# Tokens turned by VectorE and moved through DRAM instead of turned by TensorE, with the products of values as the last work of a slot

## The chip, the cores and the metric

The kernel runs on one core of a Trainium2 chip. Its time is the device time of one execution in microseconds; of several executions the median is given. The engines have separate in-order queues of instructions: TensorE (PE, with its weight loads as PEld), VectorE (DVE), ScalarE (ACT), GpSimd (POOL), and SyncE (SP), which here only issues transfers. Semaphores order instructions of different engines.

## The reference, cut to what matters

The input `x` holds 16 sequences of 256 tokens with 256 features, in float32. An attention layer and a gated feed-forward layer follow one another, each between two layer norms and with a residual:

```python
x = x + _layernorm(_L0_attn_ref(_layernorm(x), Wq, Wkv, Wkvh, Wg, Wout))
x = x + _layernorm(_L0_ffn_ref(_layernorm(x), w_gate_up, w_proj))
```

The attention has 16 heads of 128. Queries come from `Wq`; keys and values have one common part of 128 columns each (`Wkv`), which every head multiplies by its own factor per token. These factors come from `Wkvh` and, through cumulated products of sigmoids, from `Wg`, and are summed along the sequence. Queries and keys are rotated (RoPE), the scores are scaled, masked causally and put through a softmax, and the outputs of all heads go through `Wout`. The feed-forward layer multiplies by ternary weights (gate and up, 1024 hidden columns each), takes silu(gate) * up, an RMS norm, and a second ternary product.

Before both layers a product needs the normalised tokens with features along the partitions. Tokens arrive with tokens along the partitions, so they are transposed: this is the work that the change concerns.

## The kernel before, in words

Two sequences make a pair, so there are 8 pairs (class `Pair`), 16 heads each (class `Head`): 128 heads in all. Class `After` is one sequence's work after its heads: projection by `Wout`, norm, residual, feed-forward, norm, residual.

The order of all work is written out by hand. `slot(g)` (L1271) is one step for head g. It issues, in this order: steps planned for the place "first"; a load of `kh`, the factors of head g + 4 (`fetch`); the division of head g - 1's probabilities by their sums (`divide`, ScalarE, tile `even`); the scores of head g with mask and exponential (`scores`: TensorE `sps`, VectorE mask, ScalarE exponential); the turn of head g - 1's probabilities (`turn`, L631); the keys of head g + 2 (`keys`, POOL, `kT`); the queries of head g + 1 (`queries`, TensorE, `qps`); the scaled values of head g - 1 (`scale_values`, POOL, `vph`); place "scored"; the rotation of the queries of head g + 1 (VectorE: two halves of sines `turned_q`, cosines in place in `qps`, sum into `qT`); place "turned"; the reciprocals of head g's sums; place "projection"; the products of values of head g - 2 (`outputs`, TensorE, `ops`, and ScalarE's copy `oT`); places "emptied" and "last". A slot below is counted from the start of its scores on TensorE; slot 5 of a repeat of 16 means g with g mod 16 = 5.

The turn of probabilities shows the method that the change takes over for tokens. `turn` lets VectorE transpose blocks of 32x32 (`sq`), SyncE writes the result to DRAM (`moved`), and four reads, each for 32 partitions, bring the blocks where a full transposition has them (`pT`).

Everything that isn't a head's own is put into the places by `plan` methods. `Pair.plan` (L492) begins (from pair 2 on) two slots before the previous pair's first head, at slot 14 of a repeat, with `moments` (VectorE, bn_stats of `xt`), `normalise` (POOL, `xn_a`), `transpose` (TensorE, `tp_a`, into one of the four rotating PSUM buffers) and `keep` (ScalarE, into `xnT`); from `xnT` come the factors `hg` (slot 2, "last"), keys `kp` (slot 3) and values. `hg` feeds ScalarE's `gates`, first thing of slot 3. The key rotation `turned_k`, `kr` is in slot 5. `After.plan` (L1007) is called with slot 6 of a repeat for the even sequence and with slot 0 of the next one for the odd sequence: `moments`, `normalise` (`xn_f`), two slots later `transpose` (`tp_f`) and `split` (ScalarE rounds into `xhi`, VectorE subtracts into `xlo`). Then follow gates, ups and projections by `wproj_sb` (`ffn`) in the next slots, put mostly at "last" and "scored". `plan_after` (L1036) puts the projection by `Wout` (`att`), the moments of `att` (slot 3, "emptied"), the factors on POOL (slot 4, "first") and the residual: ScalarE's `y` (`add`) and POOL's sum (`add_done`, `xt`) in slots 4 to 6.

Pools: `p2` has two buffers per tag (`xn`, `sq32`, `xhi`, `xlo`, `vph`), `ps_mm` four PSUM buffers of one tag for `sps`, `qps`, `tp`, `hg`, `kp`, `gps`, `ups`, and `ps_o` one for `ops`. The last three sequences (`late`) are handled by `end` after the last slot.

Of the kernel before, what the change touches and what calls it, by code (L numbers as in the profile page):

```python
# [16 lines left out]
P = 128  # L17
# [6 lines left out]
BP = 2  # L24
# [16 lines left out]
def sandwich_kernel(  # L41
# [180 lines left out]

    class Rows:
# [35 lines left out]
        def apply(self, dst, src, engine):  # L259
            for t in range(self.count):  # L260
                engine.tensor_scalar(
                    dst[:, t, :],
                    src[:, t, :],
                    self.mv[:, t, 0:1],
                    self.rs[:, t : t + 1],
                    ALU.subtract,
                    ALU.mult,
                )

# [59 lines left out]
    class Pair:  # L329
# [7 lines left out]
        def normalise(self, b):  # L337
            self.xn[b] = p2.tile([P, 2, E], F32, tag="xn", name=f"xn_a{self.bp}_{b}")
            self.rows_of[b].factors()
            engine = nc.gpsimd if self.bp else nc.vector  # L340
            self.rows_of[b].apply(self.xn[b], xts[self.bp * BP + b], engine)
# [3 lines left out]

        def keep(self, b):
            if b == 0:
                self.xnT = p2.tile([P, EC, T], F32, tag="xnT", name=f"xnT_{self.bp}")
            nc.scalar.copy(self.xnT[:, :, b * N : (b + 1) * N], self.tp[b])
# [142 lines left out]
        def plan(self):  # L492

            end = self.bp * H
            s = end - H - (2 if self.bp > 1 else -1)
            for b in range(BP):
                put(s + b, "scored", lambda b=b: self.moments(b))
                put(s + b, "emptied", lambda b=b: self.normalise(b))
                put(s + 2 + b, "turned", lambda b=b: self.transpose(b))
                put(s + 2 + b, "emptied", lambda b=b: self.keep(b))  # L500
# [4 lines left out]
            put(s + 7, "scored", lambda: self.rope.sine(0), lambda: self.rope.sine(1))  # L505
# [205 lines left out]
    class After:  # L711
        def __init__(self, q, all_heads):
# [5 lines left out]
            self.hi_lo = {}  # L718
            self.elementwise = nc.vector if q >= B - 2 else nc.gpsimd
# [48 lines left out]
        def apply(self):  # L768
            self.xn = p2.tile([P, 2, E], F32, tag="xn", name=f"xn_f{self.q}")
            self.rows.apply(self.xn, xts[self.q], self.elementwise)  # L770

        def transpose(self):
            self.tp = transposed(self.xn, f"f{self.q}")

        def split(self):
# [4 lines left out]
            nc.scalar.copy(self.parts[0], self.tp)  # L780
            nc.vector.tensor_sub(self.parts[1], self.tp, self.parts[0].bitcast(F32))
# [225 lines left out]
        def plan(self, s):  # L1007

            put(s, "scored", self.moments)
            put(s, "emptied", self.normalise)  # L1010
            put(s + 2, "turned", self.transpose)
            put(s + 2, "emptied", self.split)
# [258 lines left out]
    def slot(g):  # L1271
# [36 lines left out]
        if 2 <= g < total + 2 and not all_heads[g - 2].on_pe:  # L1308
            all_heads[g - 2].outputs()
        fill(g, "emptied")  # L1310
        fill(g, "last")

# [42 lines left out]
```

## Time and profile before

| | |
|---|---|
| median of 3 runs | 1115.41 us (1115.2 to 1116.61) |
| the profiled execution | 1118.2 us, its span 1116.4 us |
| busy: PE / DVE / ACT / POOL | 96% / 76% / 66% / 61% |
| mean granted TensorE clock | 0.994 |
| transposes `tp_a` and `tp_f` | 64 each, 273 ns by their rows |
| VectorE's turn `sq`, 128x768 | 110, mean 974 ns |
| `pT<-moved`, issue to landing | 440, median 2.2 us |
| `moved<-sq`, issue to landing | 110, median 2.3 us |
| waits of PE for `qT` / for the reciprocal after it | 10.7 us / 7.3 us |

The span lies between the first and the last instruction; 1.8 us of the execution's time lie around it. In rows of groups, a name such as `tp_f<-ident,xn_f` is the tile written and the tiles read, then come shapes, the number of instructions, their busy time together, their mean length, and the idle time of the engine ahead of them with what ended it. Matmuls overlap, so the row's length of one is longer than what it takes from the next.

### The profile page before, as it was taken

To read this page: it belongs to the slowest core of one execution; us is meant where nothing else is said; L and a number is where in the kernel's file an instruction comes from. 1 tells how busy PE (TensorE), PEld (TensorE's weight loads), DVE (VectorE), ACT (ScalarE), POOL (GpSimd) and SP (SyncE) were. 2 spreads that over 40 slices of the span, in tenths; PEclk is the share of its full clock that TensorE was granted. 3 is DMA by queue.
4 is the path that set the end of the run, shared out by engine and by line. 5 is a ranking of instruction groups with operands and counts; after the bars stand their busy time and mean duration, and the time that the engine had idled before them with its cause. 6 is when DMAs were issued, how large, how long until landed. Compare 5 with 4: busy or idle time off the path is not lost.

```text
span 1116.4 us, 18641 instructions
## 1 busy us (share of the span) xinstructions
PE 1073.3 (96%) x5738; PEld 862.4 (77%) x5738; DVE 845.7 (76%) x2303; ACT 740.8 (66%) x2152; POOL 684.1 (61%) x757
## 2 busy tenths in 40 slices
PE   8899998999999999999999999999999999999986
PEld 5577775788778787888778887788878887788786
DVE  5878889867796777968788677877779677776365
ACT  2778766675676757767576766857567675767563
POOL 3767796438656585548665586555855465656343
PEclk9999999999999999999999999999999999999997
DMA  4512224444444444445454454444444444443101
GB/s 151 163 48 69 76 81 152 152 144 141 141 133 126 147 136 141 134 126 157 126 146 131 125 153 135 146 125 152 139 136 138 126 136 137 139 126 109 39 1 38
DMA packets 108611, 137.35 MB, mean 123 GB/s; under 512 B 12192, under 2 KB 76192, under 8 KB 108512
## 3 DMA queue, kind: packets, MB, share of 16 engines
q1 hardware_dynamic: 103344, 125.09, 36.7%
q0 software_dynamic: 2000, 6.56, 1.8%
q10 hardware_dynamic: 3168, 4.52, 1.2%
q8 instruction: 46, 0.75, 0.3%
q14 instruction: 53, 0.43, 0.1%
HBM read 88.41 MB, written 47.71 MB: 122 GB/s over the span
## 4 chain that ended last, share of the span: by engine, by line
PE 73%; DVE 14%; POOL 5%; ACT 5%; issue 2%; DMA 1%; SPq 0%; ACTq 0%; POOLq 0%; DVEq 0%
PE att L735 16%; PE qps L285 14%; PE sps L575 11%; PE ops L691 8%; PE ffn L882 6%; PE ups L789 5%; PE ops L698 4%; PE gps L789 3%; DVE turned_q L307 3%; ACT even L627 2%; DVE sq L634 2%; DVE qps L315 1%; DVE qT L318 1%; PE hg L285 1%; PE vps L285 1%
## 5 line engine op out<-in xcount | busy, mean ns | idle before, releaser
L598 ACT ACTIVATE prob<-prob,low 128x128 f32<-128x128 f32 (+1 forms) x512 | 225.8, 443 | 38.0 <-DVE low L588 37.6
L285 PE MATMUL qps<-xnT,wq_sb 128*128 128x512 f32 x512 | 240.8, 593 | 0.1
L735 PE MATMUL att<-wout_sb,oT 128*128 128x256 f32 x1024 | 239.1, 380 | 0.7 <-ACT oT L706 0.7
L735 PEld LDWEIGHTS att<-wout_sb,oT 128*128 128x128 f32 x1024 | 189.5, 190 | 40.5 <-issue 16.5
L706 ACT COPY oT<-ops 128x512 f32<-128x512 f32 x128 | 74.9, 585 | 217.8 <-PE ops L698 217.6
L588 DVE CUSTOM_DVE_ANT_0 prob<-sps,mask 128x128 f32<-128x128 f32 (+1 forms) x512 | 157.7, 352 | 79.2 <-PE sps L575 78.3
L575 PE MATMUL sps<-kT,qT 128*128 128x128 f32 (+1 forms) x1024 | 193.4, 332 | 18.3 <-DVE qT L318 10.7
L307 DVE TENSOR_TENSOR turned_q<-qps,sin_sb 64x512 f32<-64x512 f32 x256 | 176.2, 688 | 16.7 <-PE qps L285 11.4
L675 POOL TENSOR_TENSOR vph<-vp,vh 128x512 f32<-128x512 f32 x110 | 115.8, 1053 | 99.6 <-PE ops L698 99.6
L575 PEld LDWEIGHTS sps<-kT,qT 128*128 128x128 f32 x1024 | 145.8, 191 | 38.8 <-DVE qT L318 14.3
L563 POOL TENSOR_TENSOR kT<-kh,kr 128x512 f32<-128x512 f32 x128 | 165.6, 1294 | 11.7 <-PE sps L575 9.3
L627 ACT ACTIVATE even<-prob,total 128x128 f32<-128x128 f32 (+1 forms) x440 | 163.9, 446 | 6.6 <-DVE total L609 6.4
L285 PEld LDWEIGHTS qps<-xnT,wq_sb 128*128 128x128 f32 x512 | 95.9, 190 | 67.5 <-issue 61.2
L691 PE MATMUL ops<-pT,vph 128*128 128x256 f32 x440 | 131.4, 380 | 2.5 <-DMA pT<-moved 1.8
L835 POOL TENSOR_TENSOR lo<-h,hi 128x512 fp32r<-128x512 f32 x54 | 68.6, 1271 | 90.6 <-ACT hi L833 90.6
L634 DVE STREAM_TRANSPOSE sq<-even 128x768 f32<-128x768 f32 x110 | 107.2, 974 | 17.5 <-ACT even L627 16.0
L598 ACT ACTIVATION_READ_ACCUMULATOR prob<-prob,low 128x1 f32 x512 | 96.5, 189 | 0.0
L315 DVE TENSOR_TENSOR qps<-qps,cos_sb 128x512 f32<-128x512 f32 x128 | 89.6, 700 | 4.7
L698 PEld LDWEIGHTS ops<-pT,vph 128*128 128x128 f32 x440 | 83.6, 190 | 11.4
L318 DVE TENSOR_TENSOR qT<-qps,turned_q 128x512 f32<-128x512 f32 x128 | 88.6, 692 | 4.4
L853 POOL TENSOR_TENSOR squares<-squares,sq 128x512 f32<-128x512 f32 x39 | 49.9, 1279 | 66.4 <-ACT sq L852 66.4
L691 PEld LDWEIGHTS ops<-pT,vph 128*128 128x128 f32 x440 | 74.4, 191 | 14.9 <-issue 7.2
(165 smaller groups left out, 1950.4 us busy)
## 6 DMA issues: line engine op xcount, KB each, us to landing
moved<-sq SPq DMA_DIRECT2D x110, 384.0 KB, 2.3
pT<-moved SPq DMA_DIRECT2D x440, 96.0 KB, 2.2
kh<-rows SPq DMA_DIRECT2D x126, 256.0 KB, 3.4
xt<-in_x_dram SPq DMA_DIRECT2D x16, 256.0 KB, 2.9
out_dram<-y POOLq DMA_DIRECT2D x13, 256.0 KB, 3.4
wq_sb<-in_wq_dram ACTq DMA_DIRECT2D x2, 1024.0 KB, 9.6
wout_sb<-in_wout_dram ACTq DMA_DIRECT2D x1, 2048.0 KB, 15.6
w_gu<-in_wgu_dram POOLq DMA_DIRECT2D x8, 256.0 KB, 3.4
```

The costliest lines, as they stand in the source:

```text
L285: nc.tensor.matmul(ps, lhs[:, c, :], rhs[:, c, :], start=(c == 0), stop=(c == EC - 1))
L307: self.engine.tensor_mul(by_sequence(self.turned[a : a + HALF, :]), by_sequence(self.src[b : b + HALF, :]), over_sequences(sin_sb[b : b + ...
L563: nc.gpsimd.tensor_mul(self.kT, self.kh, self.pair.kr)
L575: nc.tensor.matmul(sps[:, cols], self.qT[:, n0 + i * P : n0 + (i + 1) * P], self.kT[:, n0 : n0 + (i + 1) * P], start=True, stop=True,)
L588: nc.vector.tensor_tensor_reduce(out=prob[:, cols], in0=sps[:, cols], in1=mask[:, P - i * P :], scale=-SCALE, scalar=F32_MAX, op0=ALU.add, ...
L598: nc.scalar.activation(prob[:, cols], prob[:, cols], AF.Exp, bias=low[:, i : i + 1], scale=-1.0, accum_out=self.total[:, b * 2 + i : b * 2 ...
L627: nc.scalar.activation(dst, src, AF.Copy, scale=self.total[:, 2 * b + i : 2 * b + i + 1])
L634: nc.vector.transpose(turned.rearrange("p k u q -> p (k u q)"), self.even.rearrange("p k u q -> p (k u q)"),)
L675: nc.gpsimd.tensor_mul(self.vp, self.pair.vp, self.pair.vh[:, :, self.h : self.h + 1].to_broadcast([P, NT, D]),)
L691: nc.tensor.matmul(ops[:, n0 : n0 + N], self.vp[:, b * (N // P), :], early, start=True, stop=False,)
L698: nc.tensor.matmul(ops[:, n0 + P : n0 + N], self.vp[:, b * (N // P) + 1, :], late, start=False, stop=True,)
L735: nc.tensor.matmul(self.acc[:, t, :], oT[:, n0 + t * P : n0 + (t + 1) * P], wout_sb[:, h, :], start=(h == 0 and t == 0), stop=(h == H - 1) ...
```

## The change

The tokens of pairs 2 to 7 and the feed-forward tokens of sequences 2 to 11 are no longer transposed by TensorE. POOL normalises them into a layout in which the 32x32 blocks of a 128x128 square are grouped by their place in it (`squares_first`); VectorE transposes all blocks in one instruction (`turn_rows`); SyncE writes the result to DRAM as 128 rows of four runs of 512 bytes, and one slot later four reads bring each quarter to its 32 partitions (`fetch_turned`). ScalarE copies from there, now from SBUF, in two instructions instead of one, which puts the tokens in order (`in_order`); in `split`, VectorE's subtraction is in two as well. `turned`, `moved` and `xT` share the buffers of the head's `sq32`, new DRAM buffers, and those of `xn`.

The plans move with it. Moments of pairs from 2 on, of all feed-forward sequences with such a plan, and the sines of these pairs' keys are put at "turned" rather than "scored". Of the sequences 2 to 11, an even one begins one slot earlier than before, an odd one six slots earlier. From slot 34 on, `outputs` comes after the place "last".

```diff
--- before.py
+++ after.py
@@ -220,6 +220,10 @@
             var = dst
         nc.gpsimd.tensor_tensor(dst, var, minus_half[:, : dst.shape[1]], ALU.pow)
 
+    def squares_first(xn):
+
+        return xn.rearrange("p k c t i -> p t c k i")
+
     class Rows:
 
 
@@ -258,14 +262,42 @@
 
         def apply(self, dst, src, engine):
             for t in range(self.count):
+                to, of = dst[:, t], src[:, t, :]
+                if len(to.shape) > 2:
+                    of = of.rearrange("p (c k i) -> p c k i", c=EC, i=32)
                 engine.tensor_scalar(
-                    dst[:, t, :],
-                    src[:, t, :],
+                    to,
+                    of,
                     self.mv[:, t, 0:1],
                     self.rs[:, t : t + 1],
                     ALU.subtract,
                     ALU.mult,
                 )
+
+    def turn_rows(xn, name):
+
+        turned = p2.tile([P, 4, 3 * BP, 32], F32, tag="sq32", name=f"sq32_{name}")
+        turned = turned.rearrange("p k u q -> p (k u q)")[:, : 2 * E]
+        nc.vector.transpose(turned, xn.rearrange("p k c t i -> p (k c t i)"))
+        moved = dram.tile([P, 4, P], F32, tag="xmoved", name=f"xmoved_{name}", bufs=3)
+        nc.sync.dma_start(out=moved, in_=turned.rearrange("p (k u) -> p k u", k=4))
+        return moved
+
+    def fetch_turned(moved, name):
+
+
+        xT = p2.tile([P, 4, EC, 2, 32], F32, tag="xn", name=f"xT_{name}")
+        by_square = moved.rearrange("(a j) k u -> k j a u", a=4)
+        for k in range(4):
+            nc.sync.dma_start(
+                out=xT[32 * k : 32 * k + 32].rearrange("j a c t i -> j a (c t i)"),
+                in_=by_square[k],
+            )
+        return xT.rearrange("p a c t i -> p c t a i")
+
+    def in_order(ap):
+
+        return ap.rearrange("p (t a i) -> p t a i", t=2, i=32)
 
     def tiles(ap):
         return [ap[:, t, :] for t in range(2)]
@@ -335,18 +367,34 @@
             self.rows_of[b] = Rows(tiles(xts[self.bp * BP + b]), f"a{self.bp}_{b}")
 
         def normalise(self, b):
-            self.xn[b] = p2.tile([P, 2, E], F32, tag="xn", name=f"xn_a{self.bp}_{b}")
+            turned = self.bp > 1
+            shape = [P, 4, EC, 2, 32] if turned else [P, 2, E]
+            self.xn[b] = p2.tile(shape, F32, tag="xn", name=f"xn_a{self.bp}_{b}")
             self.rows_of[b].factors()
-            engine = nc.gpsimd if self.bp else nc.vector
-            self.rows_of[b].apply(self.xn[b], xts[self.bp * BP + b], engine)
+            self.rows_of[b].apply(
+                squares_first(self.xn[b]) if turned else self.xn[b],
+                xts[self.bp * BP + b],
+                nc.gpsimd if self.bp else nc.vector,
+            )
 
         def transpose(self, b):
             self.tp[b] = transposed(self.xn[b], f"a{self.bp}_{b}")
+
+        def turn(self, b):
+            self.moved = turn_rows(self.xn[b], f"a{self.bp}_{b}")
+
+        def fetch_turned(self, b):
+            self.tp[b] = fetch_turned(self.moved, f"a{self.bp}_{b}")
 
         def keep(self, b):
             if b == 0:
                 self.xnT = p2.tile([P, EC, T], F32, tag="xnT", name=f"xnT_{self.bp}")
-            nc.scalar.copy(self.xnT[:, :, b * N : (b + 1) * N], self.tp[b])
+            dst = self.xnT[:, :, b * N : (b + 1) * N]
+            if self.bp > 1:
+                for c in range(EC):
+                    nc.scalar.copy(in_order(dst[:, c, :]), self.tp[b][:, c])
+            else:
+                nc.scalar.copy(dst, self.tp[b])
 
         def factors(self):
 
@@ -493,16 +541,22 @@
 
             end = self.bp * H
             s = end - H - (2 if self.bp > 1 else -1)
+            turned = "turned" if self.bp > 1 else "scored"
             for b in range(BP):
-                put(s + b, "scored", lambda b=b: self.moments(b))
+                put(s + b, turned, lambda b=b: self.moments(b))
                 put(s + b, "emptied", lambda b=b: self.normalise(b))
-                put(s + 2 + b, "turned", lambda b=b: self.transpose(b))
-                put(s + 2 + b, "emptied", lambda b=b: self.keep(b))
+                if self.bp > 1:
+                    put(s + 1 + b, "projection", lambda b=b: self.turn(b))
+                    put(s + 2 + b, "turned", lambda b=b: self.fetch_turned(b))
+                    put(s + 3 + b, "turned", lambda b=b: self.keep(b))
+                else:
+                    put(s + 2 + b, "turned", lambda b=b: self.transpose(b))
+                    put(s + 2 + b, "emptied", lambda b=b: self.keep(b))
             put(s + 4, "last", self.factors)
             put(s + 5, "first", self.gates)
             put(s + 5, "scored", self.raw_factors)
             put(s + 5, "last", self.keys)
-            put(s + 7, "scored", lambda: self.rope.sine(0), lambda: self.rope.sine(1))
+            put(s + 7, turned, lambda: self.rope.sine(0), lambda: self.rope.sine(1))
             put(s + 7, "emptied", self.keys_done)
             chain = end - (7 if self.bp > 1 else 8)
             put(chain - 2, "emptied", self.sigmoids)
@@ -716,6 +770,8 @@
             self.late = q >= B - 3
             self.beside = q == B - 1
             self.hi_lo = {}
+
+            self.on_pe = q < 2 or q > B - 5
             self.elementwise = nc.vector if q >= B - 2 else nc.gpsimd
 
         def buffer(self, shape, dtype, tag, name, pool=None):
@@ -766,19 +822,37 @@
             self.apply()
 
         def apply(self):
-            self.xn = p2.tile([P, 2, E], F32, tag="xn", name=f"xn_f{self.q}")
-            self.rows.apply(self.xn, xts[self.q], self.elementwise)
+            shape = [P, 2, E] if self.on_pe else [P, 4, EC, 2, 32]
+            self.xn = p2.tile(shape, F32, tag="xn", name=f"xn_f{self.q}")
+            self.rows.apply(
+                self.xn if self.on_pe else squares_first(self.xn),
+                xts[self.q],
+                self.elementwise,
+            )
 
         def transpose(self):
             self.tp = transposed(self.xn, f"f{self.q}")
+
+        def turn(self):
+            self.moved = turn_rows(self.xn, f"f{self.q}")
+
+        def fetch_turned(self):
+            self.tp = fetch_turned(self.moved, f"f{self.q}")
 
         def split(self):
             self.parts = [
                 self.buffer([P, EC, N], F32R, f"x{k}", f"x{k}", p2)
                 for k in ("hi", "lo")
             ]
-            nc.scalar.copy(self.parts[0], self.tp)
-            nc.vector.tensor_sub(self.parts[1], self.tp, self.parts[0].bitcast(F32))
+            hi, lo = self.parts
+            if self.on_pe:
+                nc.scalar.copy(hi, self.tp)
+                nc.vector.tensor_sub(lo, self.tp, hi.bitcast(F32))
+                return
+            for c in range(EC):
+                of, to = self.tp[:, c], in_order(hi[:, c, :])
+                nc.scalar.copy(to, of)
+                nc.vector.tensor_sub(in_order(lo[:, c, :]), of, to.bitcast(F32))
 
         def contract_two(self, f0, name):
 
@@ -1006,10 +1080,17 @@
 
         def plan(self, s):
 
-            put(s, "scored", self.moments)
-            put(s, "emptied", self.normalise)
-            put(s + 2, "turned", self.transpose)
-            put(s + 2, "emptied", self.split)
+
+            m = s if self.on_pe else s - 1 if self.q % BP == 0 else s - 6
+            put(m, "turned", self.moments)
+            put(m, "emptied", self.normalise)
+            if self.on_pe:
+                put(m + 2, "turned", self.transpose)
+                put(m + 2, "emptied", self.split)
+            else:
+                put(m + 1, "turned", self.turn)
+                put(m + 2, "turned", self.fetch_turned)
+                put(m + 3, ("emptied", "turned")[self.q % BP], self.split)
             if self.late:
                 return
             for u in range(FC // 2):
@@ -1305,10 +1386,13 @@
         fill(g, "projection")
         if before and before.on_pe:
             before.outputs()
-        if 2 <= g < total + 2 and not all_heads[g - 2].on_pe:
+        outputs_last = g >= 2 * H + 2
+        if 2 <= g < total + 2 and not all_heads[g - 2].on_pe and not outputs_last:
             all_heads[g - 2].outputs()
         fill(g, "emptied")
         fill(g, "last")
+        if g < total + 2 and outputs_last and not all_heads[g - 2].on_pe:
+            all_heads[g - 2].outputs()
 
     for g in range(total):
         slot(g)
```

## The prediction

> **What bounds the kernel now.** I read the page first, then starts of TensorE's instructions in order of time, then waits, then the chain that ended last in one stretch.
>
> ```profile
> PE 1073.3 (96%) x5738; PEld 862.4 (77%) x5738; DVE 845.7 (76%) x2303; ACT 740.8 (66%) x2152; POOL 684.1 (61%) x757
> ```
>
> TensorE is 96% busy, but the Trainium skill (Perfetto Trace Analysis, "Identifying the Most-Contended Engine") warns that busy time of pipelined matmuls is a bad measure. So I measured from start to start. In the timeline four transposes, one group of `tp_f`, last 0.60 us from first start to last end:
>
> ```profile
> 592.61 0.60 PE L278 MATMUL tp_f<-ident,xn_f 128*128 128x128 f32 x4
> 593.05 1.25 PE L735 MATMUL att<-wout_sb,oT 128*128 128x256 f32 x5
> ```
>
> The next product starts 0.44 us after the first transpose, so one transpose costs TensorE 0.109 us, though its own row says 273 ns. By the same reading scores take 1.31 us, queries 1.72, one head's projection 1.73, values 1.31, a group of gates or ups 0.95.
>
> I call the step of the loop over heads that begins with head g's scores slot g. From slot 34 to 111 the profile repeats every 16 slots, 131 us; I number slots in it 0 to 15. In most, slot length equals the work TensorE has in it, so TensorE bounds. Not in slots 3 to 6 (windows between score starts: length, then busy time by engine):
>
> ```profile
> 551.61:558.72 7.11, 7.11 (x33) 4.99 (x33) 5.90 (x18) 6.60 (x21) 1.99 (x8) 1.00 0.37 112
> 558.72:565.47 6.75, 6.40 (x37) 5.06 (x36) 6.57 (x22) 4.95 (x16) 5.30 (x8) 1.00 0.44 145
> 565.47:575.33 9.86, 8.97 (x44) 7.20 (x44) 6.46 (x17) 5.47 (x17) 7.53 (x7) 1.00 0.49 145
> 575.33:582.46 7.13, 7.13 (x36) 5.71 (x36) 6.98 (x21) 7.00 (x18) 2.89 (x5) 1.00 0.49 145
> ```
>
> The third column group is VectorE: 6.57 of 6.75 and 6.98 of 7.13, full. The chain shows where it comes from:
>
> ```profile
> 551.72 0.37 ACT gate L372
> ...
> 552.50 1.50 ACT even L627 x4
> ...
> 557.98 1.31 DVE st_b L232 x4
> ...
> 563.85 1.26 POOL y L948
> ...
> 567.58 1.02 ACT y L749 x2
> 568.60 1.39 ACT even L627 x4
> ...
> 570.01 0.99 DVE sq L634
> 571.02 0.69 DVE turned_k L307
> 571.73 0.68 DVE turned_k L307
> ...
> 574.59 0.70 DVE qT L318
> ```
>
> From the end of slot 2's `hg` (551.7) to the scores at 575.33 no TensorE work is on it: gates, division, turn, query rotation, moments of `att`, POOL, ScalarE, division, turn, key and query rotation. TensorE waits 0.59 us for it at slot 5 and 1.15 at slot 6.
>
> **What the skill says.** "TensorE: Matmul & The Clock Gate", Part 4: a TensorE transpose goes to PSUM and needs a copy out; about 275 ns in one kernel. The trace agrees (273), but 0.109 is what it takes from others. "VectorE: DVE Perf Modes", "The three transpose paths": VectorE turns 32x32 blocks only; hence the trip through DRAM. The row of `sq` gives its price here: 974 ns for 768 columns. "DMA: Bandwidth & Descriptors", Specifications: from 512 bytes on, transfers go at line rate. The trace has no 512-byte row of this kind; `pT<-moved` with longer runs lands in 2.2 us, `moved<-sq` in 2.3.
>
> **The change part by part.**
>
> Removed: transposes of 12 sequences of pairs 2 to 7 and of q = 2 to 11, 22 x 4 = 88 x 0.109 = 9.6 us, in slots 0, 1, 2 and 8, all TensorE-bound. Gain 9.6. Nothing but TensorE covers these.
>
> Added on VectorE: 22 turns of 512 columns, 974 x 512/768 = 0.65 us each. Two subtractions of 128x256 (426 ns, row of `y<-y,xt`) for one of 692, ten times, +0.16. All stand behind the query rotation, in slots 15, 0, 6, 8, 11, 13. At 8.7 us of slot 0 with rotation done at about 6.0 they are hidden. Slots 7 and 8 are the tightest: turn in slot 6 ends 0.55 us into slot 7, then `h` 0.69, masks 1.1, turn 0.97, rotation 2.85: about 6.7 to 6.95 of 7.0. With the 2.45 us on `gate`, slot 8 reaches 7.6 to 7.9 of 7.94. Hidden by 0.1 to 0.3 us; without cover 0.8 us a repeat.
>
> Added on ScalarE: two copies of 128x256 from SBUF (497 ns, row of `even`, which writes runs of 32 too) for one of 586, +0.4 x 22. ScalarE is 66% busy; behind the exponentials, hidden. POOL's normalising writes runs of 32: 1.22 us or, at most, double; POOL's full slots 15 and 0 lose the odd sequence's 3.4 us (in slot 0), so nothing either way.
>
> SP: a write 0.34 and four fetches 4 x 0.43 = 1.74, behind `pT` issues that end about 7.4 into a slot. Slot 1's fetch issues until 2.1 us into slot 2 and lands at 4.3; ScalarE copies until 5.2; the second sequence's `hg` starts at 6.1. Margin 0.85. The even sequence's fetch lands 5.0 into slot 8, where ScalarE comes to it at 5.4; the odd one's lands 1.8 into slot 13, before ScalarE's 3.5. The halves `xhi`, `xlo` have two buffers: an odd sequence holds one from slot 13 to slot 9, an even one from 8 to 15, so none waits. `kh` loads behind it have two slots. Traffic grows by 11.5 MB of 137 at a DMA share near 0.45.
>
> Moved, moments and key rotation: the key sines (1.39) go behind `qT` in slot 5, even moments (0.99) from slot 6 to slot 5. Slot 6 starts when slot 5's products end, about 1.0 earlier; but masks, turn and rotation of slot 6 still stand behind the same VectorE work. From `qT` of slot 5 to `qT` of slot 6 VectorE had 0.1 (reciprocal) + 1.4 (rest of the keys) + 1.1 (masks) + 1.0 (turn) + 0.96 (moments) + 2.85 (rotation) = 7.4; now the sines join: 8.8, beginning 1.4 earlier. `qT` of slot 6 comes when it came, and the stall goes on to slot 7: gain nothing. Cover gone or not, the sum is the same.
>
> Moved, values: `outputs` closes the slot. TensorE's sum is unchanged. But the copy `oT` now starts 0.2 us into the next slot (as `vp` does at slot 0, where it ends at 0.78) and stands in ScalarE's queue ahead of first copies and division. In plain slots division then ends at 2.17, when masks end too: free. In slots 0, 10 and 11, with one more copy, it is 0.45 later, under slots of 8 to 9 us: free. In slot 3 the chain above starts with two gates: now `oT` 0.58 us stands ahead of them. So +0.58 on a chain nothing covers, in five repeats: +2.9. Bounds: 0 (if TensorE's shorter order frees it) and 1.4 (this, the turn and subtractions uncovered), 0 to +7.0.
>
> Moves elsewhere: in slots 21 to 24 VectorE's order changes, not its sum: slot 21 loses 1.39 ahead of `qT` and stops at TensorE's 7.85 instead of 8.37, slot 22 is 0.15 shorter: -0.65; then the moments stand ahead of slot 23's reciprocal, its division ends 0.45 later, and slots 23 (6.24) and 24 (6.86), with under 6.5 us of TensorE work, pass that on, +0.4 each: +0.2 (-0.7 to +0.5). In slots 115 to 118 the odd subtraction no longer precedes slot 115's masks (6.93 to 6.15) and moments no longer precede slot 117's rotation (9.38 to 8.80): -1.4. In slot 125 a product waits for `y`:
>
> ```profile
> 1030.49 0.39 PE L882 MATMUL ffn<-wproj_sb,hi 128*128 128x256 f32 x1 [0.87 <-DVE y L938]
> ```
>
> Values (1.31) covered part of that wait; now they stand behind: +1.2. PSUM buffers: queries in slots 4 and 5 need the buffer of `gps`, whose copy stands behind `oT` and ends 1.26 in, queries start at 1.31: +0.5 in all (0 to 1).
>
> Sum: -9.6 + 2.9 + 0.2 - 1.4 + 1.2 + 0.5 = -6.2. The profiled execution took 1118.2 (span 1116.4), so it would take 1112.0; the median shown is 2.8 lower, one wait for `pT` of 1.0 at slot 47 among this: 1115.4 - 6.2 = **1109.2**.
>
> **Rivals.**
> A, above: own range 1106 to 1112.5. Chance 0.5.
> B, closing products cost nothing: -9.6 + 0.2 - 1.4 = -10.8, 1104.6, down to 1096 if the stalls of slots 5 and 6 go as well. For it: ScalarE is idle before `oT` for 217.8 us in all. Against: the chain begins behind `oT`. Chance 0.2.
> C, VectorE's stretch runs on through slots 7 and 8: 1.4 a repeat, 7.0 for 2.9 and 0.5: -2.6, 1112.8, to 1117. For it: the thin margins. Chance 0.18.
> D, slower: ScalarE, in order, waits in slot 2 for a late fetch, `hg` waits for its copy and TensorE with it. It begins at 0.85 us late and cancels the gain at 0.85 + 6.2/6 = 1.9; with six pairs a fetch 3 us late costs 6 x 2.15 = 12.9: 1122.1. For it: `kh` lands in 3.4, one write in 4.8. Against: median 2.2. Chance 0.12.
> The values' move could also do nothing of what it says: `pT` waits total 1.8 us, so it buys little; that is inside A and B.
>
> **How the numbers follow.** About 0.2% (2.2 us) is what a measurement here can tell: faster ends at 1113.2, slower begins at 1117.6. Faster: A 0.49, B 0.2, C 0.09: 0.78. Same: rest of A and C, 0.10. Slower: D 0.12. Range 1101 to 1117.5: leaves out B's end (0.05) and D (0.12).
>
> **What would show it.** No `tp` groups in slots 16 to 118 except for q = 0 and 1; slots 0, 1, 2, 8 each 0.44 shorter. Slot 3's division starting near 1.45 instead of 0.89; slot 5 shorter by about 1.0, slot 6 near 8.3, slot 4 near 7.3. If slots 4 to 6 sum to under 23, B; if slots 7 and 8 exceed 7.3 and 8.2, C; if `hg` waits for `xnT` over 0.5 us a pair, D. Wrong too, if a 512-column turn takes over 0.8 us or ScalarE's copies over 0.7.

## The result, and the profile after

The changed kernel takes 1122.78 us, median of ten runs (1117.18 to 1126.35); the kernel before, on the same chip, 1116.34 (1115.2 to 1117.75). The ratio is 1.0056, 95% interval 1.0038 to 1.0074: slower by 6.4 us, where 6.2 us less were forecast. The ten runs of the changed kernel lie 9 us apart, those of the kernel before 2.6; what varies between them is not shown. The profiled execution took 1121.77 us, near the median, its span 1120.0 (before: 1118.2 and 1116.4).

From the page of the changed kernel, busy time by engine and the landing of transfers:

```profile
PE 1068.9 (95%) x5650; PEld 853.0 (76%) x5650; DVE 882.3 (79%) x2335; ACT 741.0 (66%) x2174; POOL 685.9 (61%) x757
...
moved<-sq SPq DMA_DIRECT2D x110, 384.0 KB, 2.9
```

TensorE has the 88 transposes less, but VectorE has 36.6 us more, where the forecast's additions make 22 x 0.65 + 1.6 = 16. The write `moved` lands in 2.9 us by the median; it was 2.3.

As before, slots are measured from score to score. The table gives the mean length in slots 34 to 111, by place in the repeat (four or five of each). Where the forecast named no length, its column has that of before, less 0.44 in slots with transposes. The last two columns are two of the experiments below (the last is edit 7).

| slot | before | forecast | changed | subtraction on POOL | both repairs, values early in slot 2 |
|---|---|---|---|---|---|
| 0 | 9.19 | 8.75 | 8.86 | 8.86 | 8.86 |
| 1 | 7.46 | 7.02 | 7.02 | 7.02 | 7.02 |
| 2 | 8.86 | 8.4 | **9.29** | 8.70 | 8.55 |
| 3 | 7.11 | 7.1 | 7.13 | 7.13 | 7.10 |
| 4 | 6.75 | 7.3 | 7.43 | 7.43 | 6.76 |
| 5 | 9.86 | 8.9 | 8.81 | 8.81 | 8.81 |
| 6 | 7.13 | 8.3 | 8.32 | 8.33 | 8.33 |
| 7 | 7.12 | 7.1 | 7.11 | 7.11 | 7.11 |
| 8 | 8.42 | 8.0 | 7.98 | 7.98 | 7.98 |
| 14 | 8.01 | 8.0 | **8.39** | 7.98 | 7.98 |
| 15 | 8.26 | 8.0 | **8.14** | 8.04 | 8.04 |

Outside these: slots 15 to 19 grew from 39.24 to 42.63 us, slots 112 to 119 fell from 62.71 to 60.88, and slot 125 grew from 9.12 to 11.97. (At slot 15 of before, one wait of 1.0 at slot 47 is in the mean.)

Slots 3 to 6 of a repeat in the changed kernel, windows between score starts, columns as for before:

```profile
552.61:559.74 7.13, 7.13 (x34) 4.88 (x33) 5.17 (x15) 5.30 (x17) 3.63 (x9) 1.00 0.55 146
559.74:567.17 7.43, 6.73 (x37) 5.13 (x37) 7.26 (x24) 6.10 (x18) 5.29 (x8) 1.00 0.41 117
567.17:575.98 8.81, 8.80 (x44) 7.23 (x45) 5.45 (x15) 5.29 (x17) 5.50 (x5) 1.00 0.61 166
575.98:584.30 8.32, 7.20 (x38) 5.63 (x36) 8.10 (x22) 6.72 (x17) 7.58 (x8) 1.00 0.41 137
```

Slots 4 to 6 have the lengths that the forecast named. The chain that ended last, in the same repeat, has things in slots 2 and 3 that were not on before's:

```profile
547.69 1.99 DMA xT_a<-xmoved_a
...
549.75 0.41 ACT xnT L395
...
550.20 1.08 PE hg L317 x4
551.28 0.63 PE ops L745 x2
...
552.82 0.58 ACT oT L760
553.43 0.38 ACT gate L420
...
556.75 4.00 DMA moved<-sq
...
576.47 0.69 DVE turned_k L339
```

The fetch of the tokens, ScalarE's copy of it and `hg` stand on the chain in slot 2; then the products of values and `oT` ahead of the gates; then a `moved` that took 4.00 us to land.

Three places lost what was not forecast. **VectorE's subtraction.** Its row, and one pair of subtractions at the end of slot 13 with what POOL did beside it (start, length, instruction):

```profile
L855 DVE TENSOR_TENSOR xlo<-xT_f,xhi x20: 427/1392/1501, 337.1 to 904.5; 128x256 fp32r<-128x256 f32 x20
```

```profile
641.17 2.71 DVE L855 TENSOR_TENSOR xlo<-xT_f,xhi 128x256 fp32r<-128x256 f32 x2
```

```profile
640.91 1.28 POOL L909 TENSOR_TENSOR lo<-h,hi 128x512 fp32r<-128x512 f32 x1 [1.50 <-ACT hi L907]
642.15 1.45 POOL L617 TENSOR_TENSOR kT<-kh,kr 128x512 f32<-128x512 f32 x1
```

In the kernel before, one subtraction did the work of two:

```profile
L781 DVE TENSOR_TENSOR xlo<-tp_f,xhi x16: 691/692/693, 210.7 to 1071.3; 128x512 fp32r<-128x512 f32 x16
```

The two subtractions of the pair take 1.30 and 1.49 us, not 0.43. The first ends at 642.47, 0.28 us after POOL's `lo`; the second at 643.89, 0.28 after POOL's `kT`. Of the twenty, nineteen end 0.28 us or so after an instruction of POOL that was running when they began, whatever their length (0.62, 1.30, 1.49). They stand ahead of the reciprocal, the division and the masks of slot 14.

**Slot 2.** In slot 82 (starts 674.4), ScalarE and then TensorE:

```profile
681.66 0.71 ACT L395 COPY xnT<-xT_a 128x256 f32<-128x256 f32 x2 [3.34 <-DMA xT_a<-xmoved_a]
```

```profile
682.12 1.08 PE L317 MATMUL hg<-xnT,whg_sb 128*64 128x256 f32 x4 [1.34 <-ACT xnT L395]
```

ScalarE waits 3.34 us for the fetch and `hg` 1.34 for ScalarE. Slots 50, 66 and 82 lose 0.34, 1.26 and 1.56 us in this way, 3.2 in all, against the 8.58 of slot 98, which loses nothing. (In slot 34 TensorE still transposes the tokens of sequence 1, so it doesn't count here.) SyncE's issues ahead of it:

```profile
670.24 0.38 SPq L599 DMA_DIRECT2D kh<-rows  x1
670.71 0.40 SPq L695 DMA_DIRECT2D moved<-sq  x1
676.27 1.74 SPq L701 DMA_DIRECT2D pT<-moved  x4
```

`moved` goes out at 670.71, 0.47 us behind `kh`, and lands 5.5 us later; only then can the reads `pT` be issued, and behind them (678.1 to 680.0) the fetch. From this `kh` to the next, at 680.07, are 9.8 us, in a slot of 7.02.

**Slot 125 and the ternary weights.** In slot 125 the products of the last projection wait for `y`, and then:

```profile
1031.27 0.38 PE L956 MATMUL ffn<-wproj_sb,hi 128*128 128x256 f32 x1 [2.18 <-DVE y L1012]
```

```profile
1032.00:1033.00 1.00, 1.00 (x7) 1.00 (x6) 0.00 (x0) 0.00 (x0) 0.00 (x0) 0.50 0.56 169
1033.00:1034.00 1.00, 1.00 (x7) 1.00 (x6) 0.00 (x0) 0.00 (x0) 0.00 (x0) 0.50 0.00 0
```

The wait is 2.18 us instead of 0.87. In the windows the number after POOL's column is the granted TensorE clock: 0.50 after this wait. A group of `ups` took 1.7 us from first to last, instead of 0.95.

In slots 15 to 19, VectorE and POOL still make ternary weights, and pair 2's tokens come on top of them. In slot 18:

```profile
159.56 2.75 DVE L179 SCALAR_TENSOR_TENSOR t_p<-t_p 128x512 bf16<-128x512 bf16 x1 [0.63 <-POOL t_p L168]
```

```profile
166.20 0.38 PE L172 MATMUL wsum_p<-ab_p,blocks 128*128 128x512 bf16 x1 [1.94 <-ACT ab_p L158]
```

A weight step on VectorE takes 2.75 us beside POOL's `kT` and `vph`. Four such steps of the kernel before took 0.69 to 1.62 us (least, median and longest, in ns):

```profile
L179 DVE SCALAR_TENSOR_TENSOR t_p<-t_p x4: 693/992/1622, 136.3 to 166.5; 128x512 bf16<-128x512 bf16 x4
```

In the changed kernel, `ab_p` stands on ScalarE behind the copies of pair 2's tokens; TensorE waits 1.94 us for it.

### The profile page after: what moved, and what is told of

It reads as the page before. It is cut to its first block, busy times and chain, and to the rows that moved or that the text cites. A ratio compares the mean times of both kernels' runs of the same rounds, so it can differ in the third digit from the quotient of the medians.

```text
span 1120.0 us, 18737 instructions
## 1 busy us (share of the span) xinstructions
PE 1068.9 (95%) x5650; PEld 853.0 (76%) x5650; DVE 882.3 (79%) x2335; ACT 741.0 (66%) x2174; POOL 685.9 (61%) x757
## 4 chain that ended last, share of the span: by engine, by line
PE 60%; DVE 20%; ACT 8%; POOL 6%; issue 3%; DMA 3%; SPq 1%; ACTq 0%; POOLq 0%; DVEq 0%
PE att L791 13%; PE qps L317 11%; PE sps L629 9%; PE ops L745 7%; PE ffn L956 5%; DVE turned_q L339 4%; PE ups L863 4%; PE gps L863 3%; PE ops L752 3%; ACT even L681 2%; DVE sq L688 2%; DVE qps L347 2%; DVE qT L350 2%; DVE prob L642 2%; ACT prob L652 1%
## 5 line engine op out<-in xcount | busy, mean ns | idle before, releaser
L752 PEld LDWEIGHTS ops<-pT,vph 128*128 128x128 f32 x440 | 83.5, 190 | 11.7
L752 PE MATMUL ops<-pT,vph 128*128 128x128 f32 x440 | 84.5, 274 | 0.0
L956 PE MATMUL ffn<-wproj_sb,hi 128*128 128x256 f32 x256 | 76.0, 330 | 3.0 <-DVE y L1012 3.0
```

The lines of the kernel that those rows point to most:

```text
L752: nc.tensor.matmul(ops[:, n0 + P : n0 + N], self.vp[:, b * (N // P) + 1, :], late, start=False, stop=True,)
L956: nc.tensor.matmul(self.acc[:, t, :], part[:, k, t * P : (t + 1) * P], wproj_sb[:, 2 * u + k, :], start=(u == 0 and k == 0 and t == 0 and ...
```

## The experiments

Each is the changed kernel with the edit shown, if nothing else is said, and each time is compared with runs of the kernel before on the same chip. Numbers of single slots come from the profile of that kernel. Differences to the changed kernel, or from edit to edit, are often between medians of different chips; on these the kernel before took 1116.04 to 1116.92, so such a difference is uncertain by up to about 0.9 us.

**1. The subtraction on POOL.**

```diff
-                nc.vector.tensor_sub(in_order(lo[:, c, :]), of, to.bitcast(F32))
+                nc.gpsimd.tensor_sub(in_order(lo[:, c, :]), of, to.bitcast(F32))
```

> The changed kernel, but the subtraction of the feed-forward halves (xlo) is done by POOL instead of VectorE. Theory (several prices were wrong, one of them the subtraction, which with two operands in SBUF waits for POOL's instruction to end: 1.3 to 1.5 us instead of 0.43): slots 13 to 15 go from 7.02 + 8.39 + 8.13 back to about 7.0 + 8.0 + 8.05, 0.5 us in each of five repeats, so 2 to 3 us faster than the changed kernel, about 1120. Rival 'the move of the values alone is the loss': no more than 0.5 us.

1115.94 us against 1116.78, ratio 0.999 (0.9981 to 1.0). That is 6.8 us below the changed kernel, over twice what was expected. Slots 14 and 15 come back to 7.98 and 8.04, 2.5 us in five repeats, as expected. But slot 2 comes back too, to 8.58 in slots 50 and 66 and to 8.81 in slot 82, another 2.9. The trace shows the link: late subtractions made VectorE's turn of slot 14 late, so that `moved` was issued 5.5 us into the slot; with the subtraction on POOL, 3.2 us. SyncE then enters slot 0 with nothing left over (`kh` issued 0.2 us into slot 80, not 2.3), and the fetch in slot 82 is issued at 2.5, not 3.7. In this profile slot 125 also kept its clock, 1.5 us; nothing shows that the edit did that. On POOL the subtraction takes 0.73 us by the median.

**2. The subtraction on VectorE, with one input in PSUM.**

```diff
-            for c in range(EC):
-                of, to = self.tp[:, c], in_order(hi[:, c, :])
-                nc.scalar.copy(to, of)
-                nc.vector.tensor_sub(in_order(lo[:, c, :]), of, to.bitcast(F32))
+            tp = mm_tile([P, EC, N], f"tp_f{self.q}")
+            for c in range(EC):
+                nc.scalar.copy(in_order(tp[:, c, :]), self.tp[:, c])
+            nc.scalar.copy(hi, tp)
+            nc.vector.tensor_sub(lo, tp, hi.bitcast(F32))
```

> The changed kernel with one edit in split: ScalarE first copies the fetched tokens, in order, into a PSUM buffer, and from there xhi is rounded and xlo subtracted as in the kernel before; the subtraction stays on VectorE, at its place, but has one input in SBUF and one in PSUM. If it is two SBUF inputs beside POOL that stretch it, it takes 0.69 for 512 columns, slots 14 and 15 come back to 7.98 and 8.04 and slot 2 to 8.6: about 1116.5. If its place on VectorE or the layout of its input is the cause, slots 14 and 15 stay at 8.39 and 8.14: about 1122. ScalarE's two more copies of 0.4 are off the path, unless a PSUM buffer is waited for.

1116.75 us against 1116.04, ratio 1.0005 (0.9995 to 1.0015). The row of the subtraction in this kernel:

```profile
L856 DVE TENSOR_TENSOR xlo<-tp_f,xhi x10: 659/692/693, 339.0 to 901.4; 128x512 fp32r<-128x512 f32 x10
```

It is never stretched, at the same place in VectorE's order and with POOL as busy as before, and slots 14 and 15 are 7.98 and 8.04. So neither the place nor the amount of work was the cause, but two inputs in SBUF beside POOL. (The layout of the input changed with this edit too. That it wasn't the cause is shown by the changed kernel: the one subtraction that began 0.04 us before the end of POOL's instruction took 0.43 us with the same layout.) The Trainium skill says this ("SBUF — State Buffer", "Who interferes with whom"): a VectorE instruction with two SBUF inputs contends with a GpSimd instruction that reads SBUF, for ports that one of them holds alone, and the order of issue decides which is blocked. The trace agrees: in nineteen of twenty POOL's instruction had begun first, and the subtraction ended 0.28 us after it. Slot 2 came back only in part: slots 50, 66 and 82 are 8.58, 8.83 and 9.33, and `moved` of slot 78 goes out 4.45 us into its slot, between the 3.2 of edit 1 and the 5.5 of the changed kernel. The kernel before read its tokens from PSUM, at 692 ns, beside POOL or not.

**3. Pair 2's tokens on TensorE again.**

```diff
-            turned = self.bp > 1
+            turned = self.bp > 2
```

(and the same bound in `keep` and twice in `plan`)

> The changed kernel with the tokens of pair 2 transposed by TensorE in the old plan, the others turned by VectorE. Theory: slots 15 to 19, which also carry the ternary weights and grew by 3.4 us, return to the lengths of before: 3 to 4.5 us faster than the changed kernel, about 1119. Rival 'traffic' and rival 'move of the values': under 1 us, since only 2 of 22 sequences change.

1117.91 us against 1116.78, ratio 1.0014 (1.0004 to 1.0024): 4.9 below the changed kernel. Slots 15 to 19 are 39.23 us, before's 39.24 within a hundredth: 3.4 of the 4.9. The rest can't be placed by the profiles, which differ by 2.1 in all. In slot 2 two repeats still wait, up to 10.49. The edit puts this pair's moments and key sines back ahead of the rotation as well, so it shows the new plan of pair 2 as a whole to be the cause, not which part of it.

**4. Both.** Edits 1 and 3.

> The changed kernel with the subtraction for xlo on POOL and with pair 2's tokens turned by TensorE again. If the two causes are separate, the gains add: 1115.9 (subtraction on POOL alone) less 3.4 (slots 15 to 19 as before) = 1112.5. If pair 2's loss is a part of the same crowding of VectorE and POOL, less than half of the 3.4 is left: 1114.5 or more.

1112.74 us against 1116.92, ratio 0.9955 (0.9941 to 0.9969), as expected for separate causes that add. Every slot 2 from slot 50 to 98 is 8.58. Slot 125 is at 11.98 again.

**5. The products of values at their old place everywhere.**

```diff
-        outputs_last = g >= 2 * H + 2
+        outputs_last = False
```

> The changed kernel with the products of values at their old place in every slot (tokens still turned by VectorE). Theory: the copy oT leaves the head of slots 3 to 6 (0.6 us in five repeats, 3 us) and slot 125 goes back from 12.0 to about 9.1 (2.8 us); values waiting for pT may take back 1 to 2: about 4 us faster than the changed kernel, 1118 to 1119, still slower than before. Rival 'the move of the values alone is the loss': 8 us or more, to 1113 or below, faster than before.

1116.92 us against 1116.78, ratio 1.0004 (0.9991 to 1.0016). That is 5.9 below the changed kernel, more than the 4 expected, less than the 8 of the rival. 2.85 of it are slot 125, and 1.6 the last stretch after slot 127, where the clock fell later. Slots 3 to 6 gain 0.7 a repeat and slot 2 gains 0.6, but slots 8, 9 and 15 lose 0.2, 0.56 and 0.55 by the mean, because the products now wait for probabilities that come late (TensorE stands still for 0.2 to 0.8 us until `pT` has landed). In slots 8 and 9 of the kernel before, the place of the products made no difference (edit 6); with turned tokens, closing products have a use there.

**6. The closing products alone.** The kernel before, with the same move of the products as in the change.

> The kernel before, with only the products of values put last from slot 34 on; tokens are turned by TensorE as before. If that move has a cost of its own, on the chain of slots 3 to 6 (0.85 us a repeat by the trace of the changed kernel, 4.3 in five repeats) and in slot 125 (1.3 to 2.9), and wins back only the wait of 1.0 for probabilities at slot 47: +4.6 to +6.2 us, about 1122. If its cost came only from its meeting with the turned tokens (late transfers, VectorE's subtractions): within 1 us of before.

1120.82 us against 1116.92, ratio 1.003 (1.002 to 1.004): slower by 3.9, a little below the range expected. Slot 4 is 7.43 and slot 2 8.97, as in the changed kernel (6.75 and 8.86 in before): 0.8 a repeat with no turned token in the kernel; slot 125 is 10.41, +1.3, with its clock kept. Slots 47 and 115 won 1.0 and 0.8.

**7. The products early in slots 2 and 125 only.** Edits 1 and 3, and:

```diff
-        outputs_last = g >= 2 * H + 2
+        outputs_last = g >= 2 * H + 2 and not (g % H == 2 or g == total - 3)
```

> The kernel of the run before it, with the products of values at their old place in slots 2 and 125 only. If the copy oT ahead of the gates at the start of slot 3 is what lengthens the chain: 0.6 to 0.85 us less in each of five repeats, and 1.3 to 2.9 less in slot 125: 1112.5 - 2.9 to 4.3 - 1.3 to 2.9 = 1105.5 to 1108.5. If the products in slot 2 then wait for probabilities that are late, only slot 125's part is gained: 1110 to 1111.

1104.56 us against 1116.92, ratio 0.9886 (0.9873 to 0.9899): 8.2 below edit 4, a little more than expected, and the fastest of all: 1.1% faster than the kernel before. Slot 4 in its windows, the same repeat:

```profile
552.81:559.57 6.76, 6.56 (x38) 5.00 (x38) 6.61 (x22) 5.77 (x18) 5.27 (x8) 1.00 0.52 156
```

6.76, before's 6.75. With slots 2 and 3 that is 0.8 a repeat, about 4 in five, and 2.9 in slot 125. The rest is 1.2 in the last stretch, where the clock fell to 0.5 only 68.6 us after the start of slot 127 (63.0 in edit 4); this differs from profile to profile and is not counted as the edit's.

**8. The products early in slots 2 to 5 and 125.** Edits 1 and 3, and:

```diff
-        outputs_last = g >= 2 * H + 2
+        outputs_last = g >= 2 * H + 2 and not (g % H in (2, 3, 4, 5) or g == total - 3)
```

> As the run with the products of values at their old place in slots 2 and 125, now at their old place in slots 2, 3, 4, 5 and 125. If the copy oT costs on the chain only where it stands ahead of the gates (slot 3), nothing more is won, and products in slot 3 may wait for late probabilities: 1104.5 to 1107. If each oT at the start of slots 4 to 6 stands on the chain as well: up to 3 x 0.58 less in each of five repeats, 1096 to 1100.

1105.13 us against 1116.85, ratio 0.9891 (0.9877 to 0.9906): nothing more than edit 7. Slot 4 falls to 6.35, but slot 3 grows to 7.60 by waits of up to 0.48 us for probabilities, and the sum of slots 3 to 6 stays within 0.1. So taking the copy from the head of slots 4 to 6 as well wins nothing. Whether it would win something without these waits is not shown.

**9. The fetch first.** The fetch of turned tokens is put at the head of its slot.

```diff
-                    put(s + 2 + b, "turned", lambda b=b: self.fetch_turned(b))
+                    put(s + 2 + b, "first", lambda b=b: self.fetch_turned(b))
...
-                put(m + 2, "turned", self.fetch_turned)
+                put(m + 2, "first", self.fetch_turned)
```

> The changed kernel, but the four fetches of turned tokens are issued as the first thing of their slot, ahead of kh, instead of behind the pT fetches. Theory (in SyncE's order the fetch stands behind a wait for moved and so comes a slot late, ScalarE waits for it and hg with it): waits of hg for xnT go from 3 us in all to under 0.5, slot 2 of a repeat to about 8.5, 3 to 5 us faster than the changed kernel, about 1118, with less spread between executions. Rival 'added traffic makes every transfer late': moved still lands after 4 to 5 us in slots 1 and 2, hg still waits, gain under 1 us. Rival 'the move of the values is the loss': gain under 1 us.

1138.28 us against 1116.78, ratio 1.0188 (1.0166 to 1.021). The theory behind the edit was right about `hg`, which no longer waits, and wrong about the price. SyncE in slots 81 and 82 of this kernel:

```profile
681.85 0.38 SPq L283 DMA_DIRECT2D xmoved_a<-sq_a  x1
684.25 1.73 SPq L292 DMA_DIRECT2D xT_a<-xmoved_a  x4
686.07 1.28 SPq L599 DMA_DIRECT2D kh<-rows  x1
687.46 0.38 SPq L695 DMA_DIRECT2D moved<-sq  x1
691.91 1.74 SPq L701 DMA_DIRECT2D pT<-moved  x4
```

The fetch now waits in SyncE's queue for its own write, 2.0 us, with `kh` and the head's `moved` standing behind it; `moved` then needs another 4.4 us, and `pT` comes so late that the values of slot 82 wait 2.85 us. Slot 2 is 11.81 by the mean, slot 8 9.05.

**10. `kh` from POOL's queue.**

```diff
-            nc.sync.dma_start(
+            nc.gpsimd.dma_start(
                 out=self.kh,
```

> The changed kernel with one edit: the loads of kh are issued by POOL, not by SyncE. If the lateness of slot 2 is SyncE's queue, in which moved, the fetches and the turned probabilities stand one behind the other and behind kh, then moved lands sooner by up to 1 us, the fetches are issued earlier, hg's waits in slot 2 (2.9 us in all, 0.9 of it at slot 50 aside) go, and the time falls to about 1119.5. If the transfers' own time is the cause, nothing moves: 1122.8. If POOL's issue of 0.84 us in each slot delays kT and vph where POOL is full, slower: 1124 or more.

1146.25 us against 1116.92, ratio 1.0257 (1.0243 to 1.0271). It doesn't tell the two theories apart: POOL's issues, up to 0.65 us each in these slots, make it so full that the subtraction finds it busy again and again:

```profile
L855 DVE TENSOR_TENSOR xlo<-xT_f,xhi x20: 620/2111/2992, 348.1 to 927.9; 128x256 fp32r<-128x256 f32 x20
```

At 2.99 us it waits through `kT` and `vph` both, though both began after it. So in this case, unlike what the page named in edit 2 says, the order of issue did not decide. Slot 14 grows to 9.89.

**11. `kh` from ScalarE's queue.**

```diff
-            nc.sync.dma_start(
+            nc.scalar.dma_start(
                 out=self.kh,
...
-        if g + 4 < total:
-            all_heads[g + 4].fetch()
...
         fill(g, "projection")
+        if g + 4 < total:
+            all_heads[g + 4].fetch()
```

> The changed kernel with one edit: the loads of kh are issued by ScalarE, behind the rotation's place in the slot, not by SyncE at its start. If the wait of hg in slot 2 is SyncE's queue being longer than the slot, with kh ahead of moved in it, moved lands sooner, the fetches are issued sooner, and slot 2 comes to 8.6 in the four repeats from slot 66 on: 1.5 to 3 less, 1119.8 to 1121.3. If the lateness comes from the transfers' own time, or from the late turn of slot 14 alone, slot 2 stays as long as it was: 1122 to 1123.5.

Slot 2 did what the queue's theory says: 8.58 in all four repeats from slot 50 on, though slot 14 is still 8.39. The fetch of slot 82 is issued 0.7 us into it, not 3.7. The time did not: 1124.92 us against 1116.85, ratio 1.007 (1.0051 to 1.0088). ScalarE reaches the load just ahead of `moved` in slot 14, `moved` lands in 4.2 us, and the values of slot 15 wait: 9.15 by the mean instead of 8.14, and likewise in slots 23 (9.01 for 6.35) and 114. That `kh` now came from another engine's queue did not help `moved`. Nor is it the added traffic as such that makes `moved` late: in slots 1 and 2 of this kernel the turned tokens are written and fetched as before, but the last `kh` was issued over 5 us ahead, and `moved` lands in 2.3 to 3.1 us (4.0 to 5.5 in the changed kernel). The edit also moves the load to a later place in the slot, so what it shows is the distance between `kh` and `moved`, and not a merit of the queue. The Trainium skill ("DMA: Bandwidth & Descriptors", "Issuing engines are not separate DMA queues") says that transfers of all engines run on the same DMA engines and interleave; the numbers at the end of this document agree.

**12. Moments and key sines ahead of the rotation again.** Edit 7, with:

```diff
-            turned = "turned" if self.bp > 2 else "scored"
+            turned = "scored"
...
-            put(m, "turned", self.moments)
+            put(m, "scored", self.moments)
```

> The kernel with the products of values at their old place in slots 2 and 125, with the moments and the sines of the keys put ahead of the rotation of the queries again, as before. If their order is worth nothing, as the prediction had it (the stall moves from slot 6 to slot 5): slot 5 longer by 1.0 to 2.4 and slots 6 and 7 shorter by as much, 1104 to 1107. If the order behind the rotation is worth 1.0 to 1.4 in each of five repeats: 1109.5 to 1111.5.

1109.87 us against 1116.04, ratio 0.9949 (0.9934 to 0.9965): 5.3 above edit 7. That is inside the second range expected, but its reason holds only for a part: slots 5, 6 and 7 sum to 24.83, against 24.26 in edit 7, so the order is worth 0.6 a repeat, 2.9 in five, not 1.0 to 1.4. 0.6 more are in slots 112 to 119, 0.4 in slots 20 to 24, and 1.2 the clock after slot 127.

## Why the prediction was wrong

The sum was -6.2; slot by slot the profile gives about +5.0, from slot 2 on. Three steps failed. VectorE's subtraction was priced at 0.43 us and took 1.39. The fetch of the turned tokens was taken to land 4.3 us into slot 2 and landed up to 7.2 us into it, in good part because of the subtraction. And of pair 2's tokens in slots 15 to 19 the sum held only a gain of 0.9, where they cost 3.4. The forecast took the price of the subtraction from this row of the kernel before:

```profile
L981 DVE TENSOR_TENSOR y<-y,xt 128x256 f32<-128x256 f32 x6 | 2.6, 426 | 2.0 <-ACT y L973 1.9
```

By its terms:

- **The transposes, -9.6: right.** With only the values moved (edit 6) slots 0, 1 and 8 are 9.29, 7.45 and 8.41; in the changed kernel 8.86, 7.02 and 7.98. Each is 0.43 shorter.
- **VectorE's additions: the step that failed.** The turns were priced well (0.68 and 0.70 us for 0.65). The subtraction was priced at 0.43 us, by the row of `y<-y,xt`, and "+0.16" ten times was all that it was to cost; it took 1.39 us by the median, twenty times. The six of that row have both inputs in SBUF too, but they all run after 1092 us, with no instruction of POOL beside them. What the price left out is the neighbour: moving the tokens from PSUM to SBUF gave the subtraction a second SBUF input beside a busy POOL. The trace of before had the sign of it: two of the four `t_p` steps above took 0.69 us, and the other two 1.29 and 1.62 beside POOL's `vph` and `kT`. Slots 14 and 15 lost 2.5 us by the subtraction, and the delay it left in SyncE's queue was behind most of the next term (edit 1).
- **SyncE and the margin of 0.85: failed.** The forecast let the fetch be issued until 2.1 us into slot 2 and land at 4.3; in slot 82 it was issued until 5.6 and landed at 7.2. It added the new issues, but took `moved` to land as it did before, in 2.3 us; in slots 0 to 2 it took 3.3, 5.0 and 4.3 by the median, and SyncE stands still meanwhile. This is rival D's mechanism. Its price was right, one for one, but it begins later than the 0.85 worked out: fetches that landed 1.2, 1.7, 2.6 and 2.9 us after 4.3 (slots 98, 50, 66, 82) cost 0, 0.34, 1.26 and 1.56, so the margin was about 1.3. It came in three repeats and gave 3.2 us, not 12.9. That D's time, 1122.1, is close to the measured one is chance.
- **The closing products, +2.9: mechanism right, size off.** `oT` ahead of the gates costs some 0.7 in slot 4 and 0.13 in slots 2 and 3 together, about 4.1 us in five repeats (edits 6 and 7). Rival B, that they cost nothing, is out.
- **Moments and key sines, gain nothing: right in the sum, in part by luck.** Slots 5 and 6 sum to 17.13, 16.99 before, and slot 5 gave 1.05 to slot 6 as written. But in the old order (edit 12) slots 5 to 7 take 24.83, and 24.10 before: with turned tokens these slots lose 0.7, and the new order wins 0.6 of it back. The forecast had both at nothing.
- **PSUM buffers, +0.5: not seen.** In slots 66 to 82 of the changed kernel TensorE has no wait over 0.1 us ahead of the queries.
- **Rival C: out.** Slots 7 and 8 are 7.11 and 7.98.
- **Slots 21 to 24, +0.2:** they took 28.32 us for 28.60, -0.3, inside the bounds.
- **Slots 115 to 118, -1.4:** right as a sum (-1.4). But slot 115's 0.8 came with the closing products alone (edit 6), and also with the turned tokens and the products at their old place (edit 5): either is enough, and the reason given, the subtraction's new place, is not shown to be the only one.
- **Slot 125, +1.2:** the wait is worth 1.3, as said, where the clock holds (edit 6: 10.41). In the changed kernel's profile TensorE then ran at half its clock for 3.4 us, 1.5 more.
- **Slots 15 to 19, not looked at:** the forecast counted only pair 2's transposes there, -0.9; they cost +3.4. That pair 2's new plan is the cause is shown (edit 3). That it is so because VectorE, POOL and ScalarE were all busy with ternary weights is read from the waits above, and not tested by itself.

Between -6.2 and +5.0 lie 11.2 us. Slots 15 to 19 account for 4.3, slot 2 for 3.2, slots 14 and 15 for 2.5, slot 125 for 1.6 and `oT` for 1.2, together 12.8; the wait at slot 47, which is gone, gives back 1.0, and slots 21 to 24 give back 0.5. The smaller differences nearly cancel. With the subtraction, pair 2 and two slots' products repaired, the time is 1104.56: the gain from the transposes was there, and four side effects ate it.

What stays open: why the clock fell in slot 125 in some kernels and not in others with the same wait, and why SyncE was less behind before slot 98 than before slots 50 to 82. What made the difference there is `moved`: in slot 97 it went out 1.11 us behind `kh` and landed in 4.07 us, in slots 49, 65 and 81 it went out 0.47 to 0.83 behind and landed in 4.6 to 5.5.

## What to carry to other kernels

When a change moves an operand from PSUM to SBUF, price again every instruction that reads it: two SBUF inputs on VectorE next to a busy POOL cost the rest of POOL's instruction, at worst here that of two, and a detour through PSUM, or the move to the other engine, brought slots 14 and 15 back in full. A price is taken from a row only where the other engines are as busy as where it is to be used. An in-order queue that waits for landings is a resource like an engine: add up a round of it, issues and landings, and compare it with the slot before calling a transfer hidden. When a step is moved to the end of a slot, look at what heads the next slot on the engine that finishes it, slot by slot; here the same move helped in slots 8, 9 and 15 and cost in slots 2 and 125.

## What the runs showed of the hardware

- A VectorE subtraction of 128x256 with both inputs in SBUF took 0.43 us at its best, when POOL's instruction had 0.04 us left, and 0.62 to 1.50 in the other nineteen cases, which ended 0.28 us or so after POOL's instruction. With `kh` issued by POOL (edit 10) it took up to 2.99: there it ended 0.29 us after the second of two POOL instructions that had both begun later than it. On POOL it took 0.72 to 0.74, and 1.11 to 1.14 in the five cases that began during VectorE's `decay`. With one input in PSUM, 128x512 took 0.69 beside POOL.
- `moved` (384 KB) lands, in slots 34 to 111 of the changed kernel, in 2.4 us by the median (2.3 to 3.0) when the last `kh` load (256 KB, one row brought to each of 128 partitions) was issued 3 us or more ahead, and in 4.25 us (3.6 to 5.5) when it was issued less than 1 us ahead. With `kh` on ScalarE's queue the two are 2.5 and 4.3: the other queue changed neither.
- After a wait of 2.18 us in slot 125, TensorE's granted clock was 0.50 from 1032 to 1035 us in the changed kernel. After the same wait it stayed at 1.00 with the subtraction on POOL. Of the nine profiles with a wait of 2.18 us there, seven have the fall, each for 3.4 us; of the five with a wait of 0.87, none.
